# One-hots by place in a block, window sums joined on VectorE, and two smaller edits, in a four-layer graph network on one Trainium2 core

## The chip, the cores and the metric

The kernel runs on one core of a Trainium2 chip. The time is device microseconds of one execution. A core has five engines that each work through their own instructions in order: PE (matrix product), DVE (VectorE, elementwise and reductions), ACT (ScalarE, functions and copies), POOL (GpSimd; here it issues the gathers) and SP (here it only issues DMAs). PEld in the profile is PE's loading of the stationary operand. SBUF is the working memory of 128 partitions, PSUM the memory of 128 partitions and eight banks that PE writes to. Engines wait for each other through semaphores.

## The reference

Four graph layers over N = 6250 nodes of 256 features and 100,000 edges, sorted by their destination. Each layer normalizes its input by rows, applies relu, and adds its output to x:

```python
edge_index = jnp.stack([src, dst])
h = jnp.maximum(_layernorm(x), 0.0); x = x + L0(h, edge_index, ...)
h = jnp.maximum(_layernorm(x), 0.0); x = x + L1(h, edge_attr_32, edge_weight, edge_index, ...)
h = jnp.maximum(_layernorm(x), 0.0); x = x + L2(h, edge_index, edge_attr_128, ...)
h = jnp.maximum(_layernorm(x), 0.0); x = x + L3(h, edge_index, W, b)
```

What the layers have in common is a sum over the edges of a node, of rows gathered at the edges' sources:

```python
# L0, 8 heads: attention softmax over a node's edges, then projection and a feed-forward part
msg = Vh[src] * a[:, :, None];  attn = segment_sum(msg, dst);  h = x + (attn @ Wo + bo)
h = batch_norm(h); h = batch_norm(h + relu(h @ W1 + b1) @ W2 + b2)
# L1: gathered rows times filters made from 32 radial features an edge
msg = (x @ W_n2m.T + b)[src] @ W_lin1.T * (rbf @ W_r2m.T + b_r2m) * C[:, None]
out = (segment_sum(msg, dst) @ W_lin2.T + b_lin2) @ W_m2n.T
# L2, one head: a from leaky_relu(sum((x[src] + e) * attn)), softmax over a node's edges
out = relu(segment_sum(x[src] * a[:, None], dst))
# L3: rows scaled by the inverse roots of both degrees
out = relu(segment_sum((x @ W)[src] * norm[:, None], dst) + b)
```

## The kernel before

Nodes are padded to 6272 and held as NB = 49 blocks of P = 128, a block's nodes on the partitions. Edges are padded to G = 98 groups of J = 8 columns of 128 edges, so that group g holds 1024 edges, and their destinations lie within a *window* of 128 nodes: group g's window begins at node 64 g - 32 (HW = 64, OFF = 32). That is tested on the chip (`checks`, lines 261 to 267); where it holds, the function `fast` runs, otherwise `slow`, which this case does not reach. Two successive windows overlap by half.

`rel` holds each edge's place within its window (`rel = dst - first`, lines 262 and 263). A sum over edges is a matrix product: for each column j a one-hot matrix of 128 edges by 128 places (`iota == rel`) is the stationary operand and the 128 gathered rows are the moving one; the eight products of a group add up in one PSUM tile (`sum_window`, L670 in L0 and L2; L1154 in L3; in L1 the rows are stationary and the one-hots moving, L1008, so that the sum lies transposed, features on the partitions). A float32 product shows in the profile as two records of PE and two of PEld.

In L0, L2 and L3 ACT copies each window's sum to SBUF (`ws`, L672, L1158). A block of nodes needs up to four windows, since windows begin 32 nodes off the blocks' bounds and overlap. `sum_block` (L680) adds them up on PE: four products with identity matrices shifted by 32 or 96 places (`shifts`, `shift_by`, `windows_of`), in a PSUM tile T. In L1 the windows' sums are added in SBUF instead, half a window by DVE (L1035) and the other half copied by ACT (L1036), into `agg`, whose columns are nodes plus 32.

Each of the four layers ends up as a loop over g = 0 to 97 with an order written out by hand (`manual_schedule`): the order of the statements is the order of each engine's queue. In all four POOL issues eight gathers a group (L130), one for each column, 128 rows of the layer's table in HBM by the indices in `src_i`. The rows go to a ring of 6 buffers in L0 (`vrows`, in the memory of x), 12 in L1 (`hgs`, in that of `ht`), 5 in L2 and 6 in L3, and a buffer is free once the window sum that reads it has ended.

One iteration g of L0, by engine. PE: `sum_block` of the block that group g-1 completed (odd g), the output projection `project0` of the block before (even g; L780), then `of_dst(g+1)` (L743: the destinations' scores are looked up by a product of one-hots `to`, places by edges, with `scw`), the window sum of g, and the transposes of the block (L772). DVE: `logits0` (L751 to L753), `to` of g+1 (L729), the product of the rows with the exponentials (L816, in place), the block's division (`attn0`, L761 to L766), the one-hots of g+1 (L735), and the residual add with its statistics (`residual0`, L788 to L790). ACT: two exponentials (L754, L755), the copy of the window sum (L672), the copy of the transposes (`mt`, L774). SP loads `drow`, the destinations of a group on all partitions (L723). `scw` is made before the loop by products with shifted identities (L706 to L714) and `place`, the node that each partition of a window stands for, by a POOL instruction (L716), which stands in POOL's queue behind the 32 gathers of the first four groups (AHEAD = 4). PSUM's banks go to tags: S=2, A=2, T=1, B=2, E=1 in L0 (transposes and projection share B).

L1: per group three products make the filters (`filters`, L960) from `rb`, radial features of three columns on 99 partitions (33 for each, the last of 33 being ones), by a block-diagonal weight `wr3`; DVE multiplies the gathered rows by them (L1005, three instructions of 3, 3 and 2 columns), the window sum follows (L1008), DVE forms the edge term `te` (L1010, L1011), block outputs (L994), normalization, the rows of L2's table (L1026), one-hots of g+1 (L968), and at the end of the iteration adds the sum to `agg`. The radial features of two groups come by six DMAs (L949): for each third i of the partitions and each group u the columns i, i+3, i+6.

L2: DVE makes `al` (L1068 to L1070), ACT the exponential (L1072), DVE the weighted one-hots (L1075), PE the window sum; a complete block goes through `out2` (L1084 to L1090), `turned2` (L1096, L1098) and `table3_row` (L1104, L1105). L3: one-hots (L1130), window sum, and `end3` (L1136 to L1139), which adds the node's own row, scales, adds the bias and x, and stores the output.

## Time and profile before

| | |
|---|---|
| three runs | 5309.91, 5293.82, 5306.94 us; median 5306.94 |
| the profiled execution | 5323.26 us, of which the traced span is 5321.5 |
| mean granted clock of PE | 0.746 |
| busy: PE, PEld | 3068.8, 2383.4 us |
| busy: DVE, ACT, POOL | 2089.9, 609.6, 3036.3 us |
| first part (L0's table) | 0 to about 185 us |
| L0's loop; feed-forward and L1's table | to about 1425; to about 1700 us |
| loops of L1, L2, L3 | to about 3010, 4170, 5321 us |
| gathers (L130) | 3136, some 0.95 us each on POOL |

PE's records are pipelined, and their ends are modelled, so a busy PE is not PE at its peak. "remote" as the end of a wait means that the semaphore was set at a moment at which the trace shows no instruction ending that sets it. POOL's busy time is the making of a gather's descriptors, not the transfer.

### The profile page before, as it was taken

How to read it: one execution, taken by the hardware profiler on the slowest of the kernel's cores; microseconds unless marked ns; L12 is line 12 of the kernel's file. 1: busy time of each engine (PE TensorE's matmuls, PEld its weight loads, DVE VectorE, ACT ScalarE, POOL GpSimd, SP SyncE). 2: the span in 40 equal slices, each digit the busy share in tenths (PEclk: the TensorE clock that was granted, in tenths of full speed). 3: DMA queues.
4: the chain of work that ended last, by engine and by line, in shares of the span. 5: the costliest groups of instructions: out<-in, count | busy, mean ns of one | idle time of the engine just before them, and what ended most of it. 6: DMA issues, size and time to landing. Idle time of an engine off the chain costs nothing.

```text
span 5321.5 us, 42644 instructions
## 1 busy us (share of the span) xinstructions
PE 3068.8 (58%) x12132; PEld 2383.4 (45%) x12133; DVE 2089.9 (39%) x6391; ACT 609.6 (11%) x1559; POOL 3036.3 (57%) x3215
## 2 busy tenths in 40 slices
PE   7577777787896144444444545555555345554545
PEld 4366666666645133333333434444444333443334
DVE  5355555555525155555555623333333112221222
ACT  3100000000134000000000012222222100000000
POOL 0456666666203655656555266666666566666665
PEclk9777777777897567777777777777777677776777
DMA  2444444444301233333333233333333233333332
GB/s 96 124 127 139 137 141 139 139 138 136 110 0 56 60 95 100 98 103 102 97 96 103 74 96 99 97 98 100 100 99 97 76 93 99 97 97 97 98 97 84
DMA packets 258746, 536.81 MB, mean 101 GB/s; under 512 B 65096, under 2 KB 144966, under 8 KB 258502
## 3 DMA queue, kind: packets, MB, share of 16 engines
q0 software_dynamic: 137984, 364.28, 25.3%
q1 hardware_dynamic: 107750, 156.85, 9.2%
q10 hardware_dynamic: 12768, 12.85, 0.8%
q8 instruction: 103, 1.69, 0.1%
q14 instruction: 141, 1.16, 0.1%
HBM read 504.57 MB, written 29.15 MB: 100 GB/s over the span
## 4 chain that ended last, share of the span: by engine, by line
PE 35%; another core or an unknown queue 23%; issue 18%; DVE 8%; POOL 8%; ACT 5%; DMA 2%; ACTq 0%; DVEq 0%; SPq 0%; POOLq 0%
PE ps_S L670 13%; PE ps_S L1154 5%; POOL vg L130 5%; PE ps_A L743 3%; POOL big L130 3%; PE ps_T L680 3%; DVE oh L968 2%; PE ps_A L441 2%; PE ps_B L447 2%; PE ps_Q L245 1%; DVE big L1005 1%; PE ps_S L1008 1%; PE ps_B L780 1%; ACT L1072 1%
## 5 line engine op out<-in xcount | busy, mean ns | idle before, releaser
L130 POOL DMA_INDIRECT vg<-xt,src_i x1568 | 1488.6, 949 | 888.7 <-issue 543.1
L130 POOL DMA_INDIRECT big<-ht,src_i x784 | 740.4, 944 | 482.8 <-PE ps_S L1008 185.2
L130 POOL DMA_INDIRECT xbuf<-vt,src_i x784 | 764.5, 975 | 437.2 <-PE ps_S L670 191.3
L670 PE MATMUL ps_S<-vg,oh 128*128 128x258 f32 x1568 | 473.1, 467 | 435.4 <-DVE oh L1075 422.5
L680 PE MATMUL ps_T<-ws,shifts 128*128 128x265 f32 (+2 forms) x1164 | 342.4, 435 | 479.7 <-issue 319.6
L670 PEld LDWEIGHTS ps_S<-vg,oh 128*128 128x128 f32 x1568 | 371.7, 241 | 523.5 <-DVE oh L1075 436.8
L1154 PE MATMUL ps_S<-vg,oh 128*128 128x256 f32 x1568 | 431.8, 428 | 162.7 <-issue 129.3
L670 PE MATMUL ps_S<-xbuf,oh 128*128 128x265 f32 x1568 | 497.6, 480 | 20.2 <-issue 18.2
L680 PEld LDWEIGHTS ps_T<-ws,shifts 128*128 128x128 f32 x1164 | 243.0, 214 | 559.5 <-issue 397.5
L1075 DVE TENSOR_SCALAR oh<-iota,rel,ex 128x128 f32<-128x128 f32 x784 | 210.4, 359 | 662.8 <-ACT ex L1072 510.1
L1154 PEld LDWEIGHTS ps_S<-vg,oh 128*128 128x128 f32 x1568 | 342.8, 219 | 238.2 <-issue 177.1
L670 PEld LDWEIGHTS ps_S<-xbuf,oh 128*128 128x128 f32 x1568 | 371.3, 243 | 109.6 <-issue 24.8
L1130 DVE TENSOR_SCALAR oh<-iota,rel 128x128 f32<-128x128 f32 x784 | 163.1, 296 | 579.8 <-remote 413.1
L1008 PE MATMUL ps_S<-oh,big 128*128 128x128 f32 x1568 | 287.2, 357 | 172.2 <-issue 138.0
L1008 PEld LDWEIGHTS ps_S<-oh,big 128*128 128x128 f32 x1568 | 276.6, 268 | 196.8 <-issue 149.7
L994 PE MATMUL ps_B<-wout,agg 128*128 128x256 f32 x98 | 55.9, 671 | 535.0 <-DVE agg L1035 368.1
L816 DVE TENSOR_TENSOR xbuf<-xbuf,ps_E 128x2048 f32<-128x2048 f32 x98 | 223.8, 2283 | 320.6 <-issue 145.0
L743 PEld LDWEIGHTS ps_A<-scw,to 128*128 128x128 f32 x1568 | 248.7, 246 | 61.9 <-DVE to L729 45.8
L743 PE MATMUL ps_A<-scw,to 128*128 128x16 f32 x1568 | 243.8, 301 | 52.0 <-DVE to L729 48.6
L994 PEld LDWEIGHTS ps_B<-wout,agg 128*128 128x128 f32 x98 | 23.6, 299 | 553.4 <-issue 330.8
L672 ACT ACTIVATE ws<-ps_S 128x265 f32<-128x265 f32 (+1 forms) x196 | 76.3, 389 | 1702.0 <-PE ps_S L670 803.1
L960 PE MATMUL ps_A<-wr,rb 99*128 99x384 f32 (+1 forms) x588 | 207.7, 493 | 9.3 <-issue 9.3
(228 smaller groups left out, 3419.5 us busy)
## 6 DMA issues: line engine op xcount, KB each, us to landing
drow<-in_dst_row SPq DMA_DIRECT2D x98, 512.0 KB
ea<-in_edge_attr SPq DMA_DIRECT2D x98, 512.0 KB
vg<-xt,src_i POOLq DMA_INDIRECT x1568
xbuf<-vt,src_i POOLq DMA_INDIRECT x784
big<-ht,src_i POOLq DMA_INDIRECT x784
rb<-in_rbf SPq DMA_DIRECT2D x196, 49.5 KB
vt<-row SPq DMA_DIRECT2D x49, 132.5 KB
xt<-row SPq DMA_DIRECT2D x49, 129.0 KB
```

The costliest lines, as they stand in the source:

```text
L130: nc.gpsimd.indirect_dma_start(out=rows, out_offset=None, in_=table, in_offset=bass.IndirectOffsetOnAxis(ap=idx[:, j:j + 1], axis=0))
L441: nc.tensor.matmul(t[:, :n], w["w1"][:, k, m * P:(m + 1) * P], hn[:, k, :n], start=k == 0, stop=k == 1)
L447: nc.tensor.matmul(t[:, :n], w["w2"][:, m, o * P:(o + 1) * P], f[:, m, :n], start=m == 0, stop=m == 3)
L670: nc.tensor.matmul(s, oh[:, j, :], rows[:, j, :], start=j == 0, stop=j == J - 1)
L680: nc.tensor.matmul(t, shift_by(s), sums[g], start=i == 0, stop=i == len(parts) - 1)
L743: nc.tensor.matmul(dgs[g][:, j, :], tos[g][:, j * P:(j + 1) * P], scw[:, g // 2, g % 2, :], start=True, stop=True)
L816: nc.vector.tensor_tensor(vals, vals, ex[:, :, :, None].to_broadcast([P, J, H, HD]), OP.mult)
L960: nc.tensor.matmul(t, rbs[g][0:33 * n, g % 2, q, :], wr3[0:33 * n, 0:n, :], start=True, stop=True)
L1008: nc.tensor.matmul(s, hg[:, j, :], ohs[g][:, j, :], start=j == 0, stop=j == J - 1)
L1075: nc.vector.tensor_scalar(oh[:, j, :], iota, rel[:, g * J + j:g * J + j + 1], ex[:, j:j + 1], OP.is_equal, OP.mult)
L1130: nc.vector.tensor_scalar(oh[:, j, :], iota, rel[:, g * J + j:g * J + j + 1], None, OP.is_equal)
L1154: nc.tensor.matmul(s, oh[:, J - 1 - j, :], vg[:, J - 1 - j, :], start=j == 0, stop=j == J - 1)
```

## The change

`rel` becomes the place within a block, `dst & 127`, by two more operations at the end of `checks`. A window's sum therefore lies turned: row p holds the node of the window whose place in its block is p, and quarters of 32 rows belong to one block each. So no shift is needed between windows and blocks. In L0 and L2 `join` adds the quarters: where windows g-1 and g overlap, DVE adds 32 rows of the window sum g in PSUM to those of g-1, which ACT copied to SBUF (`kept`), into the block's PSUM tile T; two such adds a group, with T in two banks. The join of g-1 stands in iteration g, behind the product in L0 and behind the one-hots in L2. In L3 `add3` adds a group's sum from PSUM straight onto the nodes' own rows `rows3`, two or three adds a group, and ACT copies nothing; `end3` loses one add, and its bias comes from a PSUM tile. In L1 the sums are added to `agg` by block columns, now three operations a group alternating between one add with two copies and two adds with one.

`scw` and `place` are made by copies and small operations on ACT and DVE; `shifts` and its identity are gone. The output projection of L0 runs at every second block, for two blocks, and so does the residual add; B has one bank. The radial features of two groups come by three DMAs, each of three neighbouring columns, and the filters take the columns q, q+3, q+6.

```diff
-        ps = psc.enter_context(Psum("ps0", S=2, A=2, T=1, B=2, E=1))
+        ps = psc.enter_context(Psum("ps0", S=2, A=2, T=2, B=1, E=1))
...
+                  lambda: nc.vector.tensor_single_scalar(rel.bitcast(I32), dst_i, P - 1, op=OP.bitwise_and),
+                  lambda: nc.vector.tensor_copy(rel, rel.bitcast(I32))]
...
+        def kept(pool, s, n):
+            ws = pool.tile([P, n], F32, name="ws")
+            nc.scalar.activation(ws, s, AF.Copy)
+            return ws
+        Q = P // 4
+        def join(g, blocks, s, ws, n):
+            b = g // 2
+            quarters = [(b, 1), (b, 2)] if g % 2 else [(b - 1, 3), (b, 0)]
+            if g == G - 1:
+                quarters.append((b, 3))
+            for c, q in quarters:
+                if c < 0:
+                    continue
+                if c not in blocks:
+                    blocks[c] = ps("T", [P, n])
+                r = slice(q * Q, (q + 1) * Q)
+                if g == 0 or (g == G - 1 and q == 3):
+                    nc.vector.tensor_copy(blocks[c][r, :], s[r, :])
+                else:
+                    nc.vector.tensor_tensor(blocks[c][r, :], ws[r, :], s[r, :], OP.add)
-        def sum_block(sums, b, n):
-            t = ps("T", [P, n])
-            parts = windows_of(b)
-            for i, (g, s) in enumerate(parts):
-                nc.tensor.matmul(t, shift_by(s), sums[g], start=i == 0, stop=i == len(parts) - 1)
-            return t
...
-            place = ep.tile([P, G], F32, name="place", bufs=1)
-            nc.gpsimd.iota(place, pattern=[[HW, G]], base=-OFF, channel_multiplier=1, ...)
+            nc.scalar.activation(scw[:, :, 0, :], sc, AF.Copy)
+            nc.vector.tensor_copy(scw[:, :, 1, :], sc)
...
+            place = ep.tile([P, NB, 2], F32, name="place", bufs=1)
+            nc.vector.tensor_copy(place, nodeid[:, :, None].to_broadcast([P, NB, 2]))
...
             def project0(b):
-                t = ps("B", [P, 2, P])
+                m = mts[b // 2][:, :, 0:b % 2 + 1, :]
+                t = ps("B", [P, 2, b % 2 + 1, P])
                 for o in range(2):
                     for k in range(2):
-                        nc.tensor.matmul(t[:, o, :], w0["wo"][:, k, o * P:(o + 1) * P], mts[b][:, k, :],
+                        nc.tensor.matmul(t[:, o], w0["wo"][:, k, o * P:(o + 1) * P], m[:, k],
                                          start=k == 0, stop=k == 1)
...
-                    summed = [(b, sum_block(sums, b, VR)) for b in blocks_done(g - 1)]
-                    projected = [(b, project0(b)) for b in blocks_done(g - 2)]
+                    projected = [(b, project0(b)) for b in blocks_done(g - 2) if b % 2 or b == NB - 1]
                     if g < G:
                         ex = logits0(g)
...
                     of_dst(g + 1)
-                    for b, s in summed:
-                        attn0(b, s)
+                    if 0 < g <= G:
+                        join(g - 1, totals, sums[g - 1], kepts.get(g - 2), VR)
+                    for b in blocks_done(g - 1):
+                        attn0(b, totals[b])
                     if g < G:
-                        sums[g] = sum_window(ep, ohs[g], vg, VR)
+                        sums[g] = sum_window(ohs[g], vg, VR)
+                        kepts[g] = kept(ep, sums[g], VR)
...
                     for i in range(3):
-                        n = len(range(i, J, 3))
-                        for u in range(2):
-                            nc.sync.dma_start(rbs[g][33 * i:33 * i + 33, u, 0:n, :], rbf_v[:, g + u, i::3, :])
+                        n = min(3, J - 3 * i)
+                        nc.sync.dma_start(rbs[g][33 * i:33 * i + 33, :, 0:n, :].rearrange("c u j p -> c u (j p)"),
+                                          rbf_v[:, g:g + 2, 3 * i:3 * i + n, :].rearrange("c u j p -> c u (j p)"))
...
-                    parts[g].append((slice(3 * q, 3 * q + n), t))
+                    parts[g].append((slice(q, J, 3), t))
...
-                        if old:
-                            nc.vector.tensor_tensor(agg[:, c:c + old], agg[:, c:c + old], s[:, 0:old], OP.add)
-                        nc.scalar.activation(agg[:, c + old:c + P], s[:, old:P], AF.Copy)
+                        elif g % 2 == 0:
+                            old, new = [(c - Q, c), (c, c + Q)], [(c + Q, c + 3 * Q)]
+                        else:
+                            old, new = [(c + Q, c + 3 * Q)], [(c + 3 * Q, c + P), (c + P, c + P + Q)]
...
+            def add3(g, s):
+                b = g // 2
+                parts = [(b, Q, 2 * Q), (b, 2 * Q, P), (b + 1, 0, Q)] if g % 2 else [(b - 1, 3 * Q, P), (b, 0, 3 * Q)]
+                for c, r0, r1 in parts:
+                    if 0 <= c < NB:
+                        nc.vector.tensor_tensor(rows3[r0:r1, c, :], rows3[r0:r1, c, :], s[r0:r1, :], OP.add)
...
-                    sums[g] = ep.tile([P, D], F32, name="ws", bufs=6)
-                    nc.scalar.activation(sums[g], s, AF.Copy)
-                for b, s in summed:
-                    end3(b, s)
+                    sums[g] = s
+                if g > 0:
+                    add3(g - 1, sums[g - 1])
+                for b in blocks_done(g - 1):
+                    end3(b)
```

L2's loop is changed as L0's is: `sum_block` goes from the head of the iteration, and `join` stands before `out2`.

## The prediction

> **What bounds the kernel now.** I read the page's slices first, then the stages as windows, then who waits for whom inside a stage, then one stall in the timeline.
>
> The page's first part and its POOL and clock slices:
>
> ```profile
> PE 3068.8 (58%) x12132; PEld 2383.4 (45%) x12133; DVE 2089.9 (39%) x6391; ACT 609.6 (11%) x1559; POOL 3036.3 (57%) x3215
> POOL 0456666666203655656555266666666566666665
> PEclk9777777777897567777777777777777677776777
> ```
>
> No engine is full over the span. Four stages (L0, L1, L2, L3 below) are filled with gathers on POOL, at six tenths. The stages as windows, each split where POOL has issued its last gather (columns: stretch, its length, busy us and records of PE, PEld, DVE, ACT, POOL, granted clock, DMA share, GB/s):
>
> ```profile
> 252.00:1379.00 1127.00, 860.20 (x3789) 723.14 (x3788) 591.95 (x1626) 86.94 (x324) 717.39 (x736) 0.77 0.47 137
> 1379.00:1420.00 41.00, 38.73 (x204) 33.12 (x205) 30.53 (x83) 3.97 (x17) 0.94 (x1) 0.95 0.44 138
> ...
> 1709.00:2915.00 1206.00, 516.54 (x2243) 410.33 (x2242) 583.77 (x1458) 51.59 (x211) 732.37 (x776) 0.69 0.34 95
> 2915.00:3001.00 86.00, 61.53 (x288) 48.41 (x286) 73.59 (x186) 6.53 (x27) 0.95 (x1) 0.84 0.28 79
> 3033.00:4132.00 1099.00, 587.14 (x2142) 470.12 (x2141) 330.44 (x1353) 234.46 (x459) 730.14 (x770) 0.73 0.36 98
> 4132.00:4166.00 34.00, 23.89 (x89) 19.69 (x90) 12.92 (x53) 9.91 (x19) 1.08 (x2) 0.76 0.06 18
> 4189.00:5292.00 1103.00, 542.80 (x1882) 422.36 (x1883) 213.63 (x879) 34.89 (x93) 734.89 (x774) 0.72 0.34 98
> 5292.00:5321.00 29.00, 19.34 (x74) 15.69 (x74) 10.19 (x36) 1.87 (x5) 1.14 (x2) 0.79 0.10 31
> ```
>
> Two things are to be seen. With gathers running PE passes 3.4, 1.9, 1.9 and 1.7 matmul records per us; once they stop, 5.0, 3.3, 2.6 and 2.6. And POOL, whose gathers start 1.25 us apart, needs 98 groups x 8 x 1.25 = 980 us for a stage, while the stages take 1.1 to 1.2 ms. Who stops POOL (waits of L0, of L2, of L3; total us, times, longest):
>
> ```profile
> POOL xbuf L130 <- PE ps_S L670: 191.3, 90, 17.4
> ...
> POOL vg L130 <- remote: 145.7, 46, 5.2
> ...
> POOL vg L130 <- remote: 79.9, 25, 10.0
> POOL vg L130 <- PE ps_S L1154: 57.7, 21, 6.1
> ```
>
> POOL waits for a row buffer that PE's window sum must free. So POOL is always the full 5 or 6 buffers ahead, and PE with its partners sets the pace. "remote" is PE as well, as the timeline of L2 shows (first a pair of groups under gathers, then one after the last gather):
>
> ```profile
> 3415.33 3.65 PE L670 MATMUL ps_S<-vg,oh 128*128 128x258 f32 x16
> 3423.97 0.94 POOL L130 DMA_INDIRECT vg<-xt,src_i  x1 [0.30 <-issue]
> 3427.75 0.39 ACT L672 ACTIVATE ws<-ps_S 128x258 f32<-128x258 f32 x1 [8.78 <-remote]
> 3427.99 0.95 POOL L130 DMA_INDIRECT vg<-xt,src_i  x1 [3.08 <-remote]
> ...
> 4147.94 3.65 PE L670 MATMUL ps_S<-vg,oh 128*128 128x258 f32 x16
> 4151.62 0.39 ACT L672 ACTIVATE ws<-ps_S 128x258 f32<-128x258 f32 x1
> ```
>
> The same 16 records end 3.7 us after they start without gathers, and are seen as done 12.4 us after it with them, when POOL has run out of buffers and paused. So PE's completions arrive late under gathers, and every such lateness ends in a POOL pause.
>
> **The change, part by part.** The sum is made against the profiled execution, 5323.3 us; the median of the three runs is 16 us lower.
>
> (1) The shift matmuls (L680) go: 194 in each of L0, L2 and L3, two records each. Their busy time by stage: 96.9 + 5.9 = 103 us in L0, 87.1 + 3.8 = 91 in L2. In L3 the row says 146, but holds waits; at the L2 rate (91 / 382 records = 0.24 us) 388 records are 93, and I take 100. What of it lies on the path? Bound above: POOL's whole wait for PE goes, 191 + 146 + 138 = 475 us in the three. Bound below nothing: the matmuls lie in PE's idle time. I take PE's busy share of the stage as the share that reaches the end (860/1127 = 0.76, 587/1099 = 0.53, 543/1103 = 0.49): 78 + 48 + 49 = 175. Late next is the window sum itself, then POOL at 980 us.
>
> (2) The output projection (L780) runs for two blocks: 98 records 128x128 per bank half become half as many of 128x256, 392 to 196 (100, with the last block alone, by two). L780's records keep PE busy 74 us in L0, 0.19 each; L1104's, of the same 128x256, 51.4/196 = 0.26. 196 x 0.26 = 51, so 23 us less, x 0.76 = 17. PE waits for the turned block's copy (92.4 us, L780 <- ACT mt L774) half as often, but the copy's cover, the window sum of the next group, is the same: not counted, up to 46. With one B bank in place of two, the transposes wait for the residual add, which DVE ends before the product that the same window sum needs: nothing; without that cover the add's 0.34 us x 25.
>
> (3) The quarters are added on DVE: 2 adds a group in L0 and L2 (196 each), 243 in L3 minus 49 block adds. L761 and L1136, of 256 columns against PSUM, take 0.42 and 0.43 us. That is 82 us in L0, 82 in L2, 83 in L3. Do they wait anew? The add for group g-1 stands behind group g's product (L816) or one-hots, which wait for ACT's exponentials, and these stand behind ACT's copy of window g-1: the window is done when DVE gets there. Queued behind the add are block division, one-hots of g+1 and residual. In L0 DVE goes from 592/1127 = 53% to about 60%; the path's share is taken as PE's idle part, 0.24 x 82 = 20 (bounds 0 and 82). In L2 the normalization of a block comes 0.88 us later, 49 x 0.88 = 43; behind it ACT's next exponential waits, but in most pairs the late window sum above is later still by 8 us: 9 taken (bounds 0 and 43). In L3 DVE is busy 19%, 1.9 us of 11.3 a group; ACT's 98 copies (36.8 us) go; PE's window sum g+1 waits for the add of g-1, which ends within window g's 3.5 us: nothing (bounds 0 and 83).
>
> (4) L1 has no shift matmuls. Its sums land in blocks: 1.5 adds and 1.5 copies a group for one of each (L1035 0.21, L1036 0.22 us): 49 x 0.2 = 10 us of DVE, with DVE busy 48% of the stage: 5. The products take rows 0,3,6 / 1,4,7 / 2,5 now, so PE's second matmul waits for the second product (L1005, 0.50 us each) where three matmuls covered it: 0.3 us x 98 x 0.48 = 14 (bounds 0 and 50).
>
> (5) The radial features: 6 DMAs for a pair of groups become 3, 294 issues on SP to 147, 25,872 runs of 512 B to 9,702 of up to 1.5 KB. PE idles 9.3 us before the filters (L960), so the loads are hidden, two groups early: nothing. If the fewer packets let PE's completions through sooner, at most L1's POOL wait (185 us) comes free; nothing shows that they do.
>
> (6) L0's start. `place` is made on POOL behind 32 gathers, and DVE waits 10.8 us for it (L729); then the first logits wait 24.3 us for the lookups that started late, and POOL runs dry for 12.6. Now DVE makes it, and `scw` is copies (eight shift matmuls go, some 5 us). The first window sum comes earlier by the 10.8 at least, bounded by POOL's 12.6 idle: 12. Two more operations on `rel` (0.56 us each by L262) hide in the first stage, where DVE is busy 113 of 185 us; without that cover, 1.1 us.
>
> Sum: -175 - 17 + 20 + 9 + 5 + 14 - 12 = -156, so 5167 in the profile and 5151 for the median: I say **5150**.
>
> The granted clock speaks against part of this: 0.95 in L0's last 41 us, 0.77 before them, 0.72 in L3, where PE has more gaps. The Trainium skill, "TensorE: Matmul & The Clock Gate", section "HAM oscillation — how this bites in real kernels", gives a rule for it: gaps between matmuls beyond some 3.4 us bring the clock back to half, so a PE with less to do is partly slowed again. By that rule, with L0 falling to L3's 0.72, the 740 us of PE left in L0 grow by 7%, 51 us, x 0.76 = 39, and the sum is 5190; by the rows alone it stays at 5151, since a PE that is late less often has fewer gaps too.
>
> **Rivals.**
> - *POOL becomes the bound in L0, L2 and L3* (10%). For: PE's rate after the last gather is 1.3 to 1.5 times higher there, and 15 to 20% of records go. Against: L1, L2 and L3 have very different record counts and nearly the same period. 5307 - 475 - 12 + 19 = 4840.
> - *The gathers set the pace and the matmuls don't matter* (17%): a pause of POOL ends each stall, however much PE had to do. For: L0 with 41 records a group takes 1168/98 = 11.9 us, L3 with 20 takes 11.6. Against: the late completions come after a burst of records, and fewer of those should be late. Then only a quarter of (1) and the start come, with the costs in L1 and L2: 5307 - 44 - 12 + 28 = 5280.
> - *DVE becomes the bound in L0, slower* (19%). Its in-order work for a group (product 2.29, two adds 0.84, one-hots 1.65, half a division and half a residual 1.3, logits 0.65, `to` 0.75) is 7.5 us, more than the 6.8 a group of the last 41 us (six groups). Against: under gathers a group takes 11.9. It decides once PE's part between two window sums falls below DVE's; then all adds of L0 are on the path and so is L2's delay: 82 + 43 + 19 (L1) - 12 - 17 - 40 (the shift matmuls' own waits for ACT's copy, L680, go) = +75, 5382.
>
> **How the numbers follow.** My own case has 54%, from 5050 to 5250 (275 in place of the 175, which is six tenths of POOL's wait; or half of the 175). A measurement of this kernel tells about 0.3% (16 us) from no change. Faster: 54 + 10 and most of the second rival, 11: 0.75. Same: its rest, 0.06. Slower: 0.19. The range leaves out the far part of both outer rivals, some 2 in 10: 4930 to 5340.
>
> **What would show it.** POOL's waits for window sums in L0, L2 and L3 fall from 475 to about 300 us, and L1's stay. PE records fall from 12132 by about 1370; DVE's busy time rises by about 250 us. In L0 DVE's waits before the product (L816) stay below 320 us. The first window sum starts before 245 us. Wrong would be: POOL pauses as before with fewer records, L0 longer with DVE idle below 35%, or a clock under 0.70 in L0.

## The result, and the profile after

The changed kernel takes **5347.12 us** (median of 5, 5340.63 to 5366.02) against 5309.91 for the kernel before (median of 5, 5293.82 to 5321.62): 1.0077 times as long, 95% interval 1.0053 to 1.0101. The forecast was 5150 with a range of 4930 to 5340; it is wrong in sign. The profiled execution took 5344.24 us, its span 5342.5.

The page of the changed kernel, its first part and its POOL and clock slices:

```profile
PE 2817.9 (53%) x10760; PEld 2165.7 (41%) x10761; DVE 2337.6 (44%) x6983; ACT 573.1 (11%) x1511; POOL 3039.4 (57%) x3211
...
POOL 0456666666104655555565166666666566666665
PEclk9777777777897577777777777777777667666667
```

PE has lost 251 us and 1372 records, DVE has gained 248 us: the work moved as it was meant to. POOL's slices are as they were. The stages of the changed kernel as windows, split where POOL has issued its last gather (stretch, length, busy us and records of PE, PEld, DVE, ACT, POOL, granted clock, DMA share, GB/s):

```profile
237.00:1360.00 1123.00, 745.91 (x3245) 618.16 (x3245) 659.41 (x1754) 85.01 (x324) 721.34 (x740) 0.76 0.47 139
...
1701.00:2932.00 1231.00, 523.46 (x2234) 415.26 (x2235) 585.91 (x1500) 54.20 (x254) 732.74 (x773) 0.69 0.33 92
...
3053.00:4160.00 1107.00, 552.23 (x1776) 426.09 (x1776) 412.64 (x1541) 231.70 (x460) 729.52 (x771) 0.76 0.36 98
...
4215.00:5312.00 1097.00, 448.61 (x1520) 362.21 (x1520) 291.51 (x1067) 0.00 (x0) 734.65 (x774) 0.68 0.34 98
```

L2 and L3 have 366 and 362 PE records fewer than before and are as long: 1107 us against 1099, 1097 against 1103. POOL's waits in the changed kernel (total us, times, longest; `vg` is L2 and L3, `xbuf` L0, `big` L1):

```profile
POOL vg L128 <- remote: 290.9, 81, 10.0
...
POOL big L128 <- PE ps_S L1013: 250.2, 78, 13.1
...
POOL xbuf L128 <- PE ps_S L655: 159.7, 111, 13.6
...
POOL big L128 <- remote: 48.6, 47, 4.7
POOL xbuf L128 <- remote: 45.2, 41, 7.5
...
POOL vg L128 <- PE ps_S L1179: 3.7, 12, 0.3
```

By these rows L0, L2 and L3 wait 159.7 + 45.2 + 290.9 + 3.7 = 500 us, where the kernel before waited 191.3 + 28.5 + 225.6 + 57.7 = 503. These are the pauses that the forecast wanted to shorten to 300. They did not move.

Measured from the first matmul of a stage's window sums to the last, the two profiles differ so (us; the last row adds up to the 21 us between the spans):

| | first sum | L0 | L0 to L1 | L1 | to L2 | L2 | to L3 | L3 | end |
|---|---|---|---|---|---|---|---|---|---|
| before | 252.4 | 1167.8 | 288.6 | 1291.8 | 31.8 | 1133.6 | 22.7 | 1124.5 | 8.1 |
| after | 237.2 | 1168.4 | 295.8 | 1320.5 | 31.3 | 1136.2 | 25.4 | 1118.9 | 8.6 |
| difference | -15.2 | +0.6 | +7.2 | +28.7 | -0.5 | +2.6 | +2.7 | -5.6 | +0.5 |

So the three stages that lost their shift matmuls gained next to nothing, and L1, which had none, looks longest. Two questions follow: what sets the pace of L0, L2 and L3, and whether L1's 28.7 us are the change's.

### The profile page after: what moved, and what is told of

Its sections match the earlier page's. It is cut to its first block, busy times and chain, and to the rows that moved or that the text cites. A ratio compares the mean times of both kernels' runs of the same rounds, so it can differ in the third digit from the quotient of the medians.

```text
span 5342.5 us, 40335 instructions
## 1 busy us (share of the span) xinstructions
PE 2817.9 (53%) x10760; PEld 2165.7 (41%) x10761; DVE 2337.6 (44%) x6983; ACT 573.1 (11%) x1511; POOL 3039.4 (57%) x3211
## 4 chain that ended last, share of the span: by engine, by line
another core or an unknown queue 38%; PE 29%; DVE 14%; issue 12%; ACT 4%; POOL 1%; DMA 1%; ACTq 0%; DVEq 0%; SPq 0%; POOLq 0%
PE ps_S L655 9%; PE ps_S L1179 8%; DVE oh L973 3%; PE ps_A L741 2%; DVE big L1010 2%; DVE ea L1015 2%; PE ps_A L442 2%; PE ps_B L448 2%; PE ps_Q L243 1%; ACT L1086 1%; PE ps_S L1013 1%; DVE oh L1089 1%; POOL big L128 1%; DVE te L1016 1%
## 5 line engine op out<-in xcount | busy, mean ns | idle before, releaser
L655 PE MATMUL ps_S<-vg,oh 128*128 128x258 f32 x1568 | 517.8, 501 | 567.3 <-DVE oh L1089 430.2
L1179 PE MATMUL ps_S<-vg,oh 128*128 128x256 f32 x1568 | 461.8, 466 | 672.7 <-issue 627.0
L1179 PEld LDWEIGHTS ps_S<-vg,oh 128*128 128x128 f32 x1568 | 373.1, 242 | 761.7 <-issue 667.9
L655 PEld LDWEIGHTS ps_S<-vg,oh 128*128 128x128 f32 x1568 | 395.7, 259 | 681.1 <-DVE oh L1089 451.1
L655 PE MATMUL ps_S<-xbuf,oh 128*128 128x265 f32 x1568 | 506.2, 489 | 222.3 <-issue 221.7
L655 PEld LDWEIGHTS ps_S<-xbuf,oh 128*128 128x128 f32 x1568 | 379.0, 248 | 316.1 <-issue 229.5
L1013 PE MATMUL ps_S<-oh,big 128*128 128x128 f32 x1568 | 302.8, 364 | 191.7 <-issue 154.1
L741 PE MATMUL ps_A<-scw,to 128*128 128x16 f32 x1568 | 215.6, 281 | 98.1 <-DVE to L727 57.7
L741 PEld LDWEIGHTS ps_A<-scw,to 128*128 128x128 f32 x1568 | 217.3, 219 | 116.7 <-issue 71.4
L1031 DVE TENSOR_TENSOR row<-ps_C,bn 128x258 f32<-128x258 f32 x49 | 20.9, 427 | 490.3 <-remote 447.7
L973 DVE TENSOR_SCALAR oh<-iota,rel,cut 128x128 f32<-128x128 f32 x784 | 209.6, 348 | 0.0
```

Source lines behind the costliest of these rows:

```text
L655: nc.tensor.matmul(s, oh[:, j, :], rows[:, j, :], start=j == 0, stop=j == J - 1)
L741: nc.tensor.matmul(dgs[g][:, j, :], tos[g][:, j * P:(j + 1) * P], scw[:, g // 2, g % 2, :], start=True, stop=True)
L973: nc.vector.tensor_scalar(ohs[g][:, j, :], iota, rel[:, c], w1["cut"][:, c], OP.is_equal, OP.mult)
L1013: nc.tensor.matmul(s, hg[:, j, :], ohs[g][:, j, :], start=j == 0, stop=j == J - 1)
L1179: nc.tensor.matmul(s, oh[:, J - 1 - j, :], vg[:, J - 1 - j, :], start=j == 0, stop=j == J - 1)
```

## The experiments

Eighteen kernels ran, in five sets; each set shares its runs of the kernel before. One thing has to be known to read the numbers. The same kernel before takes 5255 to 5310 us in some sets and 4499 to 4511 us in others, with nothing in between, and within a set all kernels go together:

| set | the kernel before (runs) | gathers of L2 and L3 |
|---|---|---|
| result | 5309.91 (5) | with pauses of POOL |
| A: half_sums, half_gathers, rests, deep_L3 | 5265.45 (1) | with pauses |
| B: radial_old, radial_alone, projection_single, place_alone | 4501.52 (33) | none |
| C: changed_again, radial_old_2, both_old, evenly | 4498.66 (27) | none |
| D: to_split, to_act, to_act_old | 5255.02 (11) | with pauses |
| E: changed_3, before_again, projection_single_2 | 4511.3 (27) | none |

Sets A and B ran on a chip of the same number, ten minutes apart. What makes a set one or the other no run shows. Kernels are compared within a set alone. The kernels of set A and `evenly` ran once each.

### Does PE's work set the pace? Set A

`half_sums` takes half of PE's window sums of L2 and L3 away:

```diff
-            for j in range(J):
-                nc.tensor.matmul(s, oh[:, j, :], rows[:, j, :], start=j == 0, stop=j == J - 1)
+            for j in range(J - m, J):
+                nc.tensor.matmul(s, oh[:, j, :], rows[:, j, :], start=j == J - m, stop=j == J - 1)
...
-                        sums[g] = sum_window(oh, vgs[g], TR)
+                        sums[g] = sum_window(oh, vgs[g], TR, J // 2)
...
-                    for j in range(J):
+                    for j in range(J // 2):
```

> The changed kernel, with the window sums of L2 and L3 over four of the eight columns alone: half of their matmuls are left out, all gathers stay. First window sum to last in the changed kernel: L2 1136 us, L3 1119 us. If PE's work sets the pace (the prediction's step 1), the 259 us and 231 us of PE that go shorten L2 and L3 by about half of that each, 130 and 115 us, and POOL's pauses shrink with them. If the gathers set the pace, both stages stay within 15 us of 1136 and 1119 and POOL pauses as before.

It took 5261.3 us beside 5265.45. Its L2 and L3, gathers running (columns as above):

```profile
3011.00:4102.00 1091.00, 421.17 (x1024) 288.88 (x1024) 413.43 (x1541) 237.40 (x463) 730.98 (x770) 0.62 0.37 99
4153.00:5239.00 1086.00, 307.95 (x776) 216.32 (x776) 297.37 (x1090) 0.00 (x0) 739.62 (x774) 0.60 0.34 99
```

From first sum to last, L2 is 1117.5 us. In deep_L3 of the same set, whose L2 is the changed kernel's, it is 1119.1: 131 us of PE less in the window than in the result's profile bought 1.6 us. L3 is 1097.1, where the two other kernels of the set with all matmuls and gathers have 1112.5 and 1116.4: 141 us bought 15 to 19, not the 115 expected. (The 259 and 231 us of PE that the expectation names did not all go, since a record that is left took 0.41 and 0.40 us in place of 0.31 and 0.30.) Against 1136 and 1119 us, which are of another set, the two stages are 19 and 22 us shorter: a little more than the 15 that the expectation allowed the gathers, and far from 130 and 115. PE was idle 61% and 72% of these windows and POOL paused all the same. PE's work does not set the pace of L2 and L3 here.

`half_gathers` does the opposite: four of eight gathers a group in L2 and L3, all matmuls, each gathered column read twice.

```diff
-                for j in range(J):
+                for j in range(J // 2, J):
                     gather(vgs[g][:, j, :], xt2, src_i[:, g * J:(g + 1) * J], j)
```

> The changed kernel, with only four of the eight gathers of a group in L2 and L3; all window sums stay and read the four gathered columns twice. If PE's work sets the pace, L2 and L3 stay within 3 per cent of 1136 and 1119 us, and POOL waits for the rest. If the gathers hold PE's completions back, both fall to the larger of POOL's 98 x 4 x 1.25 = 490 us plus pauses and PE's pace after the last gather (6.7 and 4.2 us a group, 657 and 412 us): L2 to some 660, L3 to 500 to 560, and the kernel to about 4300 us.

It took 4455.93 us, 810 less than the kernel before. L2 and L3, gathers running:

```profile
3020.00:3818.00 798.00, 528.00 (x1765) 402.87 (x1766) 416.05 (x1622) 232.29 (x456) 361.41 (x383) 0.80 0.26 71
3874.00:4428.00 554.00, 394.52 (x1487) 323.68 (x1488) 286.99 (x1055) 0.00 (x0) 372.08 (x386) 0.84 0.36 103
```

PE passes in 554 us of L3 nearly what took it 1097 in the result's profile (1487 records, 1520). L3 from first sum to last is 571 us, where rests and deep_L3 have 1112.5 and 1116.4, and POOL's gathers there are 560.7 / 391 = 1.43 us apart on average. With eight a group it was 1109.7 / 783 = 1.42 in the result's profile, and 1098.0 / 783 = 1.40 in half_sums. So in a set with pauses a gather of L3 costs 1.40 to 1.43 us, whether PE has 8, 16 or 32 records to do for eight of them. L2 fell to 834 us and not to 660, which is 2.07 us a gather, and POOL waited 301 us there for window sums (L655): with half its gathers L2 has another bound, which was not followed. In L0 and L1, where the profiles with pauses have 1.48 to 1.60 us a gather, no run took matmuls or gathers away.

`rests` and `deep_L3` ask whether the pauses could be had cheaper. The first lets POOL do an unused operation after each group in L2, after every second group in L3; the second gives L3 four banks for window sums and four one-hot buffers.

```diff
+                nc.gpsimd.iota(rest, pattern=[[1, 512]], base=0, channel_multiplier=0,
+                               allow_small_or_imprecise_dtypes=True)
```

```diff
-                    s = ps("S", [P, D])
+                    s = ps("SB"[g % 2], [P, D])
...
-                        oh = one_hot3(g + 1)
+                        ohs.append(one_hot3(g + 3))
...
-                if g > 0:
-                    add3(g - 1, sums[g - 1])
+                if g > 2:
+                    add3(g - 3, sums[g - 3])
```

> The changed kernel, where POOL rests by doing an unused operation of about 1.0 us: after every group of 8 gathers in L2, after every second group in L3. Now POOL pauses some 2.9 us after 16 gathers in L2 and 5.7 us after 32 in L3, and PE's completions are seen in these pauses. If any short stretch without a gather lets them through, L2 goes from 22.9 us for two groups to about 22.0 (minus 45 us) and L3 from 45.5 for four to about 42 (minus 85 us). If the pause has to be as long as it is, the rests come on top: L2 plus 98 us, L3 plus 49 us. If PE's work sets the pace, POOL's pauses shrink by what the rests take and nothing changes.

> The changed kernel, with four banks for window sums and four one-hot buffers in L3 in place of two and two, and the adds three groups behind in place of one. If PE is held because only two window sums may be under way unseen, it passes more groups in each pause and POOL pauses less: L3 falls from 1119 us to 1000 to 1060. If the gathers set the pace whatever stands ready, L3 stays within 15 us of 1119.

`rests`: 5270.69 us, L2 1130.8, L3 1112.5; the operation took 0.58 us, not 1.0, and lengthened the gap after a group by some 0.45. What POOL's intervals exceed 1.26 us by adds up to 129.5 us in L2 and 123.0 in L3, rests included; in the changed kernel's first profile it was 143.7 and 130.3. The rests were neither added to the pauses nor did they shorten the stage: POOL merely waited that much less. The expectation had given this outcome to PE's work as the pace-setter; `half_sums` speaks against that, so `rests` shows only that POOL's own issuing does not set the pace either. `deep_L3`: 5277.57, L3 1116.4, and the same excess adds up to 122.1 us. Neither more room for PE nor short breaks change the 1.40 to 1.43 us in L3.

### Sets without pauses: B, C and E

Sets B and C were meant for the parts of the change. `radial_old` puts the loads and the columns back (first diff), `radial_alone` makes that one edit of the change in the kernel before, `projection_single` undoes the double projection (second), `both_old` undoes both, and `place_alone` is the kernel before with `place` made on DVE (third):

```diff
-                        n = min(3, J - 3 * i)
-                        nc.sync.dma_start(rbs[g][33 * i:33 * i + 33, :, 0:n, :].rearrange("c u j p -> c u (j p)"),
-                                          rbf_v[:, g:g + 2, 3 * i:3 * i + n, :].rearrange("c u j p -> c u (j p)"))
+                        n = len(range(i, J, 3))
+                        for u in range(2):
+                            nc.sync.dma_start(rbs[g][33 * i:33 * i + 33, u, 0:n, :], rbf_v[:, g + u, i::3, :])
...
-                    parts[g].append((slice(q, J, 3), t))
+                    parts[g].append((slice(3 * q, 3 * q + n), t))
```

```diff
-                    projected = [(b, project0(b)) for b in blocks_done(g - 2) if b % 2 or b == NB - 1]
+                    projected = [(b, project0(b)) for b in blocks_done(g - 2)]
```

```diff
-            place = ep.tile([P, G], F32, name="place", bufs=1)
-            nc.gpsimd.iota(place, pattern=[[HW, G]], base=-OFF, channel_multiplier=1,
-                           allow_small_or_imprecise_dtypes=True)
+            place = ep.tile([P, NB, 2], F32, name="place", bufs=1)
+            nc.vector.tensor_scalar(place[:, :, 0], nodeid, float(OFF), None, OP.subtract)
+            nc.vector.tensor_scalar(place[:, :, 1], nodeid, float(OFF), None, OP.add)
```

> The changed kernel with L1's radial loads and the order of its products as before (rows 0, 3, 6 of a DMA, products by three neighbouring columns); all else as changed. The profiles show L1 28.7 us longer after the change (1291.8 to 1320.5). If the new order of the products is what holds PE (the prediction's 14 us, bound 50), this kernel is 14 to 30 us faster than the changed one, at or a little under the kernel before. If the aggregates kept in blocks cost it, or if the 28.7 us are L1's own spread from run to run, it stays at the changed kernel's time, 0.8 per cent over before.

> The kernel before with the new radial loads and order of products alone. Order of products as the cause: 14 to 30 us slower than before (0.3 to 0.6 per cent). Loads hidden and order hidden: within 0.2 per cent of before. If fewer, longer packets let the gathers go faster: faster, at most by L1's POOL wait of 185 us.

> The changed kernel with L0's output projection one block at a time again, in the one bank that the change leaves it. The prediction gave the double projection minus 17 us by PE's share. If the gathers set the pace of L0, it gives nothing in L0, and its double residual comes last of all in L0's tail, where nothing covers it: then the single one is 0 to 8 us faster than the changed kernel. If PE's work reaches the end, it is 17 us slower.

> The kernel before with place made by two additions on VectorE in place of an operation on POOL behind 32 gathers, and nothing else. The prediction's step 6: 11 to 12 us faster than before (0.2 per cent), the first window sum at about 241 us in place of 252. If POOL's gathers set L0's end anyway, an earlier first sum only makes POOL's first pause shorter by as much, which is the same 12 us; if L0's pace takes it back, nothing.

> The changed kernel itself, as it is, beside the kernel before. In one set of runs the kernel before took 5265 us, with pauses of POOL in every stage, and in another 4501 us, with none. If POOL's gathers are the bound wherever there are no pauses, changed and before are within 0.1 per cent there; where there are pauses, the changed kernel is again 0.3 to 1.0 per cent slower, if the first result was its own and not the spread of one set of runs.

> The changed kernel with L1's radial loads and product order as before, once more. In a set of runs without pauses: as the kernel before, within 0.1 per cent, as it was. In a set with pauses: if the product order is what made L1 28.7 us longer, it is 0.3 to 0.6 per cent faster than the changed kernel of the same set; if not, equal to it.

> The changed kernel with L1's radial loads and product order as before and L0's output projection one block at a time: what is left is the one-hots in blocks, the quarters added on VectorE and the earlier start of L0. Without pauses: within 0.1 per cent of before. With pauses: if L1 and L0's tail are what the change costs (28.7 and 7 us), it is at the kernel before or up to 15 us under it by L0's earlier start.

All of these ran without pauses. L3 of the changed kernel in the result's profile, where POOL stops for a buffer (timeline: start, length, engine; in brackets the idle time before and what ended it):

```profile
4605.27 0.95 POOL L128 DMA_INDIRECT vg<-xt,src_i  x1 [0.30 <-issue]
4611.40 1.68 DVE L1149 TENSOR_SCALAR oh<-iota,rel 128x128 f32<-128x128 f32 x8 [22.99 <-remote]
4611.64 0.94 POOL L128 DMA_INDIRECT vg<-xt,src_i  x1 [5.42 <-remote]
...
4614.09 13.35 PE L1179 MATMUL ps_S<-vg,oh 128*128 128x256 f32 x48 [19.99 <-issue]
```

The timeline of L3 in `changed_again`, the same kernel in set C:

```profile
4006.36 1.66 DVE L1149 TENSOR_SCALAR oh<-iota,rel 128x128 f32<-128x128 f32 x8 [6.67 <-PE ps_S L1179]
...
4008.17 0.94 POOL L128 DMA_INDIRECT vg<-xt,src_i  x1 [0.30 <-issue]
4009.42 0.95 POOL L128 DMA_INDIRECT vg<-xt,src_i  x1 [0.30 <-issue]
...
4009.84 6.58 PE L1179 MATMUL ps_S<-vg,oh 128*128 128x256 f32 x16 [3.52 <-DMA vg<-xt,src_i]
```

In the first DVE and POOL wait for a "remote" release: a completion of PE that is seen when POOL has stood still for five microseconds. The trace's records of the semaphore that PE's products set show what is late. PE's last record before the stall ends at 4594.1 us (4614.09 less 19.99). The semaphore rises at 4593.82, 4599.41, 4604.31 and 4609.21, some 5 us apart; the last packet of a gather ends at 4607.7, and from 4611.34 to 4611.68 the semaphore rises nine times, 0.04 us apart. Then DVE and POOL go on, and PE after DVE's one-hots. In the second PE's completion is seen at once (its sixteen records before this stretch end at 4006.32), POOL never stops, and it is PE that waits, for the gathered rows. The two kinds of trace differ in one more thing: each of the nine with pauses lacks 17 to 24% of the updates of this semaphore (`after`: 3219 records for 4216 products that set it), and none of the eleven without pauses lacks any. So whether the recording of a run has a part in the pauses is open too. The stages of `before_again` as windows, from the first sum to POOL's last gather, columns as above:

```profile
231.00:1204.00 973.00, 835.46 (x3963) 703.50 (x3964) 610.02 (x1699) 97.65 (x338) 746.00 (x745) 0.85 0.55 165
1507.00:2480.00 973.00, 644.73 (x2519) 484.31 (x2517) 663.37 (x1639) 58.06 (x238) 736.53 (x776) 0.75 0.45 124
2517.00:3490.00 973.00, 608.32 (x2198) 479.39 (x2199) 348.26 (x1392) 247.22 (x473) 735.52 (x771) 0.79 0.41 111
3521.00:4494.00 973.00, 590.34 (x1934) 465.33 (x1934) 226.26 (x909) 37.26 (x97) 737.09 (x774) 0.80 0.38 111
```

The same windows of `changed_again`:

```profile
219.00:1198.00 979.00, 763.02 (x3386) 634.32 (x3386) 686.67 (x1830) 97.01 (x338) 749.52 (x754) 0.82 0.56 165
1503.00:2470.00 967.00, 627.47 (x2507) 488.76 (x2508) 664.19 (x1679) 60.82 (x285) 731.71 (x773) 0.77 0.45 124
2507.00:3475.00 968.00, 545.68 (x1824) 416.54 (x1825) 432.19 (x1584) 248.09 (x473) 730.57 (x771) 0.78 0.42 112
3508.00:4478.00 970.00, 561.61 (x1552) 431.60 (x1552) 301.83 (x1102) 0.00 (x0) 734.55 (x774) 0.75 0.38 111
```

Four stages of nearly one length, with PE busy from 56% to 86%: 98 x 8 gathers x 1.25 us = 980 us. What these edits move beside the gathers is hidden. The measurements say the same of the parts that were taken apart:

| kernel | ratio to before | 95% interval |
|---|---|---|
| changed_again, set C | 1.0002 | 0.9993 to 1.0011 |
| changed_3, set E | 0.9998 | 0.9989 to 1.0007 |
| before_again, set E | 1.0000 | 0.9991 to 1.0009 |
| radial_old, radial_old_2 | 0.9995, 1.0002 | 0.9986 to 1.0004, 0.9993 to 1.0011 |
| radial_alone | 1.0003 | 0.9994 to 1.0012 |
| projection_single, projection_single_2 | 0.9998, 0.9994 | 0.9989 to 1.0007, 0.9985 to 1.0003 |
| both_old | 0.9998 | 0.9989 to 1.0007 |
| place_alone | 1.0003 | 0.9994 to 1.0012 |

What `place_alone` shows is the plainest case of a gain that does not arrive. The first window sum comes at 217.8 us, and at 231.4 in `radial_alone`, which leaves L0 as it was. The last window sum of L0 comes at 1216.1 and 1215.4. POOL's gathers of L0 begin at 180 to 182 us in both and take 1023 and 1020 us. They set the end of L0, and an earlier start of the sums only makes PE wait longer for rows.

Two small terms do recur in nearly every profile. With the new radial loads and product order the stretch from L0's last sum to L1's first is 293.6 to 296.5 us (thirteen profiles), with the old ones 288.6 to 291.5 (seven): some 5 us, in a stretch where no gathers run; whether the loads or the order of the products cost it was not followed. And from L2 to L3 the kernel before takes 22.0 to 22.8 us, and most variants of the changed one 24.5 to 27.

`evenly` tests the bound from the other side, by an unused POOL operation after each gather of L3:

```diff
                         gather(vg[:, j, :], xt3, src_i[:, g * J:(g + 1) * J], j)
+                        nc.gpsimd.iota(rest, pattern=[[1, 256]], base=0, channel_multiplier=0,
+                                       allow_small_or_imprecise_dtypes=True)
```

> The changed kernel, where POOL does an unused operation of about 0.33 us after every gather of L3, so that gathers start some 1.44 us apart in place of 1.25. If PE's completions are late because gathers come faster than the chip takes them in (1.42 us each over the pauses of the first profile), then in a set with pauses they are on time here, POOL waits no more, and L3 is 98 x 8 x 1.44 = 1129 us, where it was 1119 with the pauses. If the lateness goes with any gather that is under way, POOL pauses as before and L3 is over 1200 us. In a set without pauses L3 is 1129 us against 979.

It took 4688.37 us. A stretch of the timeline of its L3:

```profile
4011.57 0.36 POOL L1176 IOTA rest<- 128x256 f32 x1
4012.09 0.96 POOL L128 DMA_INDIRECT vg<-xt,src_i  x1 [0.16 <-issue]
4013.05 0.37 POOL L1176 IOTA rest<- 128x256 f32 x1
...
4013.52 5.89 PE L1182 MATMUL ps_S<-vg,oh 128*128 128x256 f32 x16 [5.07 <-DMA vg<-xt,src_i]
4013.58 0.96 POOL L128 DMA_INDIRECT vg<-xt,src_i  x1 [0.16 <-issue]
```

The gathers start 1.49 us apart, and L3 grows from 979 to 1168 us, which is 784 x 1.49: POOL's time is the stage's time, one to one. The set had no pauses, so the other half of the question (whether evenly spaced gathers keep PE's completions on time where there are pauses) was not answered.

### Touching the bound: set D

In `changed_again`, without pauses, L0 is 989 us from first sum to last where the other stages are 972 to 979. About one gather in each of its groups is longer:

```profile
701.96 0.75 DVE L727 TENSOR_SCALAR to<-drow,place 128x1024 f32<-128x1024 int32 x1
702.07 1.45 POOL L128 DMA_INDIRECT xbuf<-vt,src_i  x1 [0.30 <-PE ps_S L655]
```

In this profile the gathers of L0 that overlap `to` in time take 1.27 us on average, and the median of all is 0.95; in L1 to L3, beside the one-hots of 128 columns, they take 0.96. The Trainium skill, "SBUF — State Buffer", section "SBUF: two separate sides", has the rule for it: some VectorE operations hold the port that GpSimd needs to write the descriptors of its DMAs, and the gather stands until they end. The two rows agree with it: this gather starts 0.11 us after `to`, overlaps it for 0.64 us and takes 0.50 us more than the median. Three kernels take the long operation away: into eight pieces of 128 columns, or to ScalarE as a square and a cut at zero, the last one without the double projection and the new radial loads.

```diff
-                    nc.vector.tensor_scalar(tos[g], drows[g], place[:, g:g + 1], None, OP.is_equal)
+                    for c in range(0, J * P, J * P // 8):
+                        c = slice(c, c + J * P // 8)
+                        nc.vector.tensor_scalar(tos[g][:, c], drows[g][:, c], place[:, g:g + 1], None, OP.is_equal)
```

```diff
-                    nc.vector.tensor_scalar(tos[g], drows[g], place[:, g:g + 1], None, OP.is_equal)
+                    nc.scalar.activation(tos[g], drows[g], AF.Square, bias=place[:, g:g + 1], scale=1.0)
+                    nc.scalar.activation(tos[g], tos[g], AF.Relu, bias=ones_c, scale=-1.0)
```

> The changed kernel with L0's lookup one-hots (to, L727) made in eight pieces of 128 columns in place of one of 1024. In a set without pauses, one gather of each L0 group takes 1.3 to 1.45 us in place of 0.95, and it is the one that lies beside this operation of 0.75 us; 36 us of POOL's time in L0 go there. If VectorE's long operation holds the gather up, pieces of 128 columns (0.2 us each) do so less: L0's gathers end up to 32 us earlier and the kernel is up to 0.7 per cent faster than before. If the gather loses the same time to each piece, or if VectorE (0.7 busy there, 0.9 us a group more by this) becomes L0's bound, nothing is gained or L0 grows.

> The changed kernel with the same one-hots made on ScalarE, as a square of the difference and one minus it cut at zero, two operations of some 1.1 us a group on an engine that is busy a tenth of L0. If VectorE's operation is what holds one gather of each group up, L0's 36 us of lengthened gathers go and the kernel is 30 to 36 us faster than before, 0.7 to 0.8 per cent, where there are no pauses. If the lengthening belongs to the group's first product or to PE, nothing changes. With pauses in the set: gathers are taken in at 1.42 us each whatever POOL does, and the gain is lost.

> The same one-hots on ScalarE, and with them L1's radial loads and product order as before and L0's output projection one block at a time. Without pauses the two reversals gave nothing alone (0.9998), so it is equal to the kernel with the one-hots on ScalarE within 0.1 per cent. With pauses: if L1's 28.7 us and L0's tail of 7 us belong to these two edits, it is 0.5 to 0.7 per cent faster than the other.

The group of L0's gathers on the page of the result's profile (busy us, mean ns; idle before):

```profile
L128 POOL DMA_INDIRECT xbuf<-vt,src_i x784 | 764.9, 976 | 417.6 <-issue 176.4
```

The same group of `to_split`:

```profile
L128 POOL DMA_INDIRECT xbuf<-vt,src_i x784 | 746.8, 953 | 439.6 <-PE ps_S L655 169.5
```

And of `to_act`:

```profile
L128 POOL DMA_INDIRECT xbuf<-vt,src_i x784 | 745.2, 951 | 508.0 <-issue 427.7
```

The lengthening is gone in both, so `to` as one long operation was its cause; beside the pieces a gather takes 0.96 us. Why the pieces, 0.28 us each and together longer than `to`, do not hold gathers up as much was not followed. But this set had pauses, and nothing was gained: `to_split` 5296.89 us (1.0076, 1.0058 to 1.0095), `to_act` 5357.03 (1.0196, 1.0172 to 1.0219), `to_act_old` 5331.3 (1.0137, 1.0113 to 1.0161). What POOL saved in the gather came back as idle time before it. `to_act` is slower in L0 (1246.5 us against 1180.9 in `to_split`): its two operations take 1.14 us each where DVE took 0.75 for one, and the lookups wait for both; that this is the whole reason was not shown. Whether `to_split` gains its up to 32 us in a set without pauses was not run.

The last two differ by 26 us, as expected for L1 and L0's tail, but not there: with the old radial loads L1 is longer (1283.6 against 1265.8), and it is L0 that is shorter by 38 us. So the radial edit is not what makes L1 long in this set; that its sums go to block columns was undone in no run. In the six other profiles with pauses that have the changed L1 it takes 1286, 1293, 1276, 1276 (set A), 1279 and 1266 us (set D), so one and the same L1 differs by 17 us within a set; the 1320.5 of the first profile stands alone. They are less on average than the 1291.8 of the kernel before, but that is one profile of another set, and in sets A and D the kernel before was 45 to 55 us faster and was not profiled. Whether the change makes L1 longer where gathers pause is therefore not shown either way.

> The changed kernel as it is, for its time and stages beside the kernel before of the same set. Without pauses: within 0.1 per cent of before, as it was. With pauses: seven profiles of kernels with the changed L1 put it at 1266 to 1293 us but for the first one, 1320.5, against 1291.8 before. If that first one was spread, L1 is 1265 to 1295 here and the kernel 0.1 to 0.5 per cent over before; if L1 is what the change costs, L1 is over 1300 and the kernel 0.6 to 1.0 per cent over.

> The kernel before against itself: a ratio of 1 within 0.1 per cent, and a second profile of its stages. With pauses, its L0, L1, L2 and L3 show how far stages move from run to run without any change: if L1 comes out between 1265 and 1280 here, the 28.7 us of the first pair of profiles cannot be read as the change's; if it is 1290 again, the changed L1 is no longer than before's in the other profiles either.

> The changed kernel with L0's output projection one block at a time. Without pauses: as before, within 0.1 per cent. With pauses: with the one-hots on ScalarE, the single projection went with an L0 of 1209 us against 1247. If the double projection, its copies and its residual come late there by themselves, this kernel is 10 to 40 us faster than the changed one (0.2 to 0.7 per cent); if that came only from ScalarE being filled, equal to it.

This last set, meant to compare these in the presence of pauses, had none; its ratios are in the table above. **What stays open**: which part of the change makes it 0.8% slower where gathers pause. It is measured once for the kernel itself, and once as 0.76% for it with `to` in pieces; in set A two kernels with all its matmuls and gathers, rests and deep_L3, were 5 and 12 us over the one run of the kernel before. The terms that recur (5 us before L1, 3 us before L3) are a fifth of the 37 us between the medians. Without pauses they are made up for at L0's end: the last window sum comes at 1208 to 1213 us with the changed L0 and at 1215 to 1218 with the old one, also with `place` alone; which edit does that was not followed. The double projection is a suspect after set D, not shown. No version beats both kernels: `projection_single_2`, at 0.9994, can't be told from no change.

## Why the prediction was wrong

**What bounds the kernel** is where it went wrong first. "PE with its partners sets the pace" was read from POOL's waits: POOL is always as many buffers ahead as it has, so PE must be the slower. The rows were right and the conclusion was not. PE's completions are seen late while gathers run, and the buffer waits for the completion. Halving PE's window sums left the pauses in L2 and L3; halving the gathers halved L3; without pauses PE waits for the rows. The line that said so was in the forecast, as the second rival's "for": 11.9 us a group in L0 with 41 records, 11.6 in L3 with 20. Equal periods under unequal work are what a common pace-setter looks like.

**(1) The shift matmuls, -175.** This is the step that failed. "I take PE's busy share of the stage as the share that reaches the end": with the costs of (3) in them, L0 and L2 came out 0.6 and 2.6 us longer and L3 5.6 us shorter, and in half_sums 131 and 141 us less of PE were worth 1.6 and 15 to 19. The bound below, nothing, was about the value. The rows that it should have been priced from were the pauses' own: in the changed kernel 143.7 us over L2's 783 intervals and 130.3 over L3's, 0.18 and 0.17 us for each gather, and 0.16 and 0.15 in half_sums, with half the products.

**(2) The double projection, -17.** Nothing without pauses (undoing it: 0.9998 and 0.9994); with pauses it was not run alone.

**(3) The quarters on DVE, +29.** DVE's 248 us came as worked out, but no stage is longer by as much as was put down for it (20, 9 and 0): as far as the two terms can be told apart, these adds lie under the gathers too.

**(4) L1, +19.** The first pair of profiles shows +28.7 and seems to confirm it; by the spread of the others it is not shown either way. Without pauses L1 is 972 us changed and 977 before. There the wait of the second matmul for the second product costs nothing in the loop, where PE waits for rows anyhow.

**(5) The radial loads, 0.** Right in the loop; some 5 us were overlooked at L1's start, where no gather covers it.

**(6) L0's start, -12.** The first sum came 15 us earlier (11 to 14 without pauses), as said. In the one pair of profiles with pauses L0's last sum is earlier by as much (1420.2 to 1405.6); without pauses `place` alone gave nothing at L0's end.

**The rivals.** "The gathers set the pace and the matmuls don't matter" is what happened in L2 and L3, the stages that were tested, at 17% and with the wrong price: it still let a quarter of (1) and the start's 12 us through, and so stood at 5280. The same sum with nothing of (1) is 5307 - 12 + 28 = 5323, 24 us under the result. "POOL becomes the bound", 4840, had the right floor of 980 us a stage, but PE's matmuls are not what lies between the kernel and that floor. DVE is busy at most 70% of a stage in the windows above (L0 of `changed_again`), and nothing points to it as the bound. Among the signs named in advance, "POOL pauses as before with fewer records" came true.

**The clock.** The Trainium skill's rule that gaps bring PE's clock down ("TensorE: Matmul & The Clock Gate", "HAM oscillation — how this bites in real kernels") agrees in direction: in L3 the granted clock is 0.72 before, 0.68 after, 0.60 with half the sums and 0.84 with half the gathers. It priced a loss of 39 us in L0, where the clock went from 0.77 to 0.76 and the length stayed. Here a slower PE cost nothing, since its work didn't set the pace.

## What to carry to other kernels

An engine that is always its full number of buffers ahead need not be faster than its consumer: it may be waiting for a signal that its own traffic holds up, so look whether the consumer is busy in that time, and compare stages with unequal work. If their period per transfer is the same, price an edit first by the transfers that it takes away, put work beside them near nothing, and count what lies outside the loops (here 5 us before L1) in full. Then test it: with the gathers halved L2 met another bound, and with pauses `to` made on ScalarE left L0 66 us longer than `to` in pieces on VectorE. And a difference of one stage between two profiles, like L1's 28.7 us here, is a cause only if a second pair shows it.

## What the runs showed of the hardware

- One program on one core has two paces, 5255 to 5310 and 4499 to 4511 us, for whole sets of runs, also on a chip of the same number ten minutes apart. In the slower one eight gathers a group cost 1.40 to 1.44 us each in the long run in L2 and L3, against 1.25 to 1.26. The gathers' DMA packets are no slower in it: 152 to 154 ns each in L3 in both.
- In the slower pace updates of PE's semaphore are seen some 5 us apart while gathers run, up to 17 us after PE's last record, and 0.04 us apart once the gathers' packets have ended (one stall of L3 in the result's profile). The traces of this pace lack 17 to 24% of these updates.
- In L3 in that pace the average holds with half the matmuls, twice the banks and breaks of 0.58 us. What holds the completions up, and why a set has one pace or the other, no run shows.
- A gather beside a VectorE operation over 1024 columns of SBUF (0.75 us) takes 1.27 us on average in place of 0.95 in `changed_again`, and 1.13 in the result's profile, with pauses; beside pieces of 128 columns (0.28 us) it takes 0.96 in `to_split`, with pauses too.
